# A planned GNN kernel: the planner's delay behind the GpSimd norm offsets, one planned cost, and the list of random moves are changed

## The chip, the cores and the metric

The kernel runs on one core of one Trainium2 chip. The metric is the device time of the whole program in microseconds. Three runs of the kernel before the change took 1513.4, 1514.27 and 1516.3 us; their median is 1514.27 us. A separate execution was recorded by the hardware profiler.

## What is computed

The input is 32 samples of 512 nodes with 128 features, and one adjacency matrix of 512 by 512 that all samples share. Four layers follow one another, each of them `x = x + layer(relu(layernorm(x)))`:

```python
    # layer 0: graph convolution
    A_hat = adj + eye; d = sum(A_hat, -1) ** -0.5
    out = einsum('nm,bmc->bnc', d[:, None] * A_hat * d[None, :], h) @ W.T + b
    # layer 1: gated graph network, five steps, in_matrix = out_matrix = adj
    m = einsum('nm,bmd->bnd', adj, h); av = concatenate([m, m])
    z = sigmoid(av @ w3.T + b3 + h @ u3.T + c3); r = sigmoid(av @ w4.T + b4 + h @ u3.T + c3)
    hv = tanh(av @ w5.T + b5 + (r * h) @ u5.T + c5); h = (1 - z) * h + z * hv
    # layers 2 and 3: graph attention over the edges of adj; layer 2 ends in elu
    h = x @ W; e = leaky_relu((h @ a_src)[:, None] + (h @ a_dst)[None, :])
    out = softmax(where(edge, e, -inf)) @ h
```

The layernorm has no learned scale: it is `(x - mean) / sqrt(var + eps)` over the 128 features. It stands ahead of every layer, so that there are four of them for each sample.

## The kernel before, in words

**Tiles.** A sample is one tile of 128 partitions by 4 chunks by 128 features (512 numbers in a partition). A product with the adjacency matrix (`in_three`, L682) and with the gate weights (`by_m`, L798) is done in three one-pass matmuls over an upper part, a lower part and a cross term. Between the second and the third of them ScalarE multiplies the accumulated PSUM bank by a constant (`rescale`, L664): TensorE can't go on in that bank until this is done. `operands` (L655 on ScalarE, L656 and L658 on VectorE) splits a value into the three parts. `weigh` (L795) holds the full-precision gate products, `step` the five steps of layer 1 (L828, L835 and L839 are their tanh on ScalarE; L830, L841, L842 and L844 are the elementwise work on VectorE), and `shuttle` and `shuttle_first` (L632, L642) turn a tile by a VectorE transpose and a pass through DRAM. `gat` is an attention layer: scores (L927), head values (L931), the masked exponentials on VectorE (L954), the weighted sum on TensorE (L980), its reciprocal (L983) and the residual (L987 to L1013).

**The norm.** `norm_relu` serves almost all norms. VectorE takes statistics of the four chunks (`bn_stats`, L546) and combines them (`bn_aggr`, L550). GpSimd then runs four operations on tiles of 128 by 4: variance plus eps (L558), its power -0.5 (L559), the negated mean (L560), and the product of the two last, the offset (`off`, L563). ScalarE then does one activation for each chunk: `relu(rstd * x + off)` (L565). Its output `y` or `h` goes to `operands`, to a VectorE transpose, or to a product. The first sample has a norm of its own (`norm_first`), and so have the attention layers of the last four samples (`center_relu`, L601 to L612): there ScalarE subtracts the mean only (L609), `aggr` (L605, L606) is on VectorE, and GpSimd's power (L612) is used later, on the attention scores.

**What sets the order.** Nothing runs in the order in which the Python code states it. Every operation is registered with `op(engine, cost, due, emit, r, w, delay)`: an engine, a cost in microseconds, a due time, what it reads and writes, and the delay from its end to the moment at which an operation that depends on it may start. Where no delay is given, one for each engine is used: 0.1 us for GpSimd, 0.145 for VectorE, 0.15 for ScalarE. `Plan.run` simulates the engines with these numbers: at each moment an engine takes, of its operations that are ready, the one with the smallest `soon`. It repeats the simulation ten times from each of two starting points, with `soon` replaced by the latest time that a backward pass allows, and keeps the best. Then `nudge` shifts the `soon` of some operations by the list `NUDGES`, `attempt` simulates once more, and the instructions are emitted in the order that comes out. On the chip each engine runs its own instructions strictly as emitted and waits on semaphores; the planner's times are not used there. Buffers are given out by the same simulation, so another order gives other buffers too.

**The random moves.** Each number of `NUDGES` stands for one move. A hash of it gives a window of planned time (20 to 800 us wide), the share of operations in the window that are touched, and how far their `soon` may be shifted at random, up or down:

```python
            width = 20 * 40 ** a
            begin, share, far = b * (end + width) - width, 65536 * 0.01 ** c, 0.02 * 100 ** d
```

One unit of `soon` is a slot of 9.7 us of planned time. The hash uses the number of the operation in the order of registration. Moves touch nothing that was planned in the first 12 us.

Of the kernel before, what the change touches and what calls it, by code (L numbers as in the profile page):

```python
# [14 lines left out]
ALU = mybir.AluOpType  # L15
# [14 lines left out]
WHOLE_GATES = {(0, 0), (1, 0)}  # L30

NUDGES = (
    582105, 147139, 36044, 562756, 451743, 52419, 574539, 43563, 131, 944493, 237051, 489767, 324034, 993924,
    895393, 724877, 242989, 757855, 969479, 343813, 441295, 487621, 599115, 887003, 965300, 304846, 630193,
    477347, 598911, 606866, 611222, 822063, 367989, 367611, 600045, 340292, 705911, 227256, 683560, 256619,
    236075, 331440, 177108, 65046, 739182, 728740, 720890, 134124, 359225, 176816, 49127, 311405, 367939,
    434468, 67122, 748109, 340066, 705658, 439275, 222157, 242131, 988248, 71674, 381732, 216141, 968473, 71317,
    32857, 119823, 447754, 129853, 185381, 116398, 835989, 550221, 241039, 261563, 95546, 93460, 950398, 27867,
    697942, 355550, 295201, 292698, 219542, 683929, 109572, 242409, 593734, 360934, 635653, 959394, 718615,
    571381, 736407, 37849, 298732, 275792, 981235, 444799, 634242, 442703, 439138, 943350, 210407, 114489,  # L40
    768468, 744083, 634443, 397291, 8136, 704668, 301010, 180477, 60933, 775473, 129214, 351397, 904571, 88879,
    916910, 435502, 757825, 84502, 678117, 887492, 424299, 920868, 742722, 635518, 887601, 436851, 937755,
    981183, 211427, 823433, 130707, 279663, 792970, 259083, 204724, 504719, 754655, 308189, 858342, 979517,
    719747, 751352, 82391, 821335, 468677, 957002, 276599, 466154, 75528, 451824, 370167, 884142, 189521,
    257883, 334963, 165897, 278684, 456540, 104146, 215128, 931617, 11886, 964863, 855753, 469785, 705445,
    36320, 949458,
)


# [29 lines left out]
class Plan:  # L79
# [13 lines left out]
    def op(self, engine, cost, due, emit, r=(), w=(), delay=None):  # L93
        o = Op(engine, cost, due, emit, self.DELAY[engine] if delay is None else delay)
        o.id = len(self.ops)
        before = {}
        for items, writes in ((r, False), (w, True)):
            for item in items:
                v, parts = item if isinstance(item, tuple) else (item, None)
                parts = range(len(v.writers)) if parts is None else [parts]  # L100
                if v not in o.vals:
                    o.vals.append(v)
                    v.uses += 1
                for c in parts:
                    before.update((p.id, p) for p in v.writers[c])
                    if writes:
                        before.update((p.id, p) for p in v.readers[c])
        for items, writes in ((r, False), (w, True)):
            for item in items:
                v, parts = item if isinstance(item, tuple) else (item, None)  # L110
                for c in range(len(v.writers)) if parts is None else [parts]:
                    if writes:
                        v.writers[c], v.readers[c] = [o], []
                    else:
                        v.readers[c].append(o)
        before.pop(o.id, None)
        for p in before.values():
            p.then.append(o)
        o.waits = len(before)
        self.ops.append(o)  # L120
# [190 lines left out]
def gnn_stack(ctx: ExitStack, tc: tile.TileContext, a: dict, out: bass.AP):  # L311
    nc = tc.nc
# [49 lines left out]
    op = plan.op  # L362
# [45 lines left out]
    for c in range(C):  # L408
        e, q = (("ACT", nc.scalar), ("SP", nc.sync))[c % 2]
        op(e, 0.45, -1001, lambda c=c, q=q: q.dma_start(adj_sb.t[:, c, :], adj[c * P:(c + 1) * P, :]),  # L410
           w=[adj_sb[c]], delay=(3.2, 4.7, 4.4, 4.9)[c])
# [42 lines left out]
    for m in range(C):  # L454
        op("DVE", 0.26, -800 + 0.7 * m, lambda m=m: nc.vector.tensor_add(diag.t[:, m, :], block(adjT.t, m), ident.t),
           r=[adjT, ident], w=[diag[m]])
# [67 lines left out]
    for k, u, half in (("w4", "u3", True), ("w3", "u3", True), ("w5", "u5", False)):  # L524
        gate_b[k] = fixed([P, 1], "gate_b" + k)
        op("DVE", 0.1, -14, lambda k=k, u=u: nc.vector.tensor_add(gate_b[k].t, raw["b" + k].t, raw["b" + u].t),
           r=[raw["b" + k], raw["b" + u]], w=[gate_b[k]])
# [4 lines left out]
    for i, l in enumerate((2, 3)):  # L532
        p = Val("bank")
        op("PE", 0.3, 9, lambda i=i, l=l, p=p: nc.tensor.matmul(p.t[:, 0, :2], gats.t[:, i, :], a_pair[l].t, start=True, stop=True),
           r=[gats, a_pair[l]], w=[p])
# [7 lines left out]
    def norm_stats(b, due):  # L543
        xb, st, mv = xs[b], Val("st", C), Val("mv")
        for c in range(C):
            op("DVE", 0.196, due, lambda c=c: nc.vector.bn_stats(st.t[:, c, :], xb.t[:, c, :]), r=[xb[c]], w=[st[c]])  # L546

        def aggr():
            for c in range(C):
                nc.vector.bn_aggr(mv.t[:, c, :], st.t[:, c, :])  # L550
        op("DVE", 0.29, due, aggr, r=[st], w=[mv])
        return mv

    def norm_relu(b, y, due, times=None):

        xb, off, rstd = xs[b], Val("off"), Val("rstd")
        mv = norm_stats(b, due)
        op("POOL", 0.5, due, lambda: nc.gpsimd.tensor_tensor(rstd.t, mv.t[:, :, 1], eps.t, ALU.add), r=[mv, eps], w=[rstd])  # L558
        op("POOL", 1.15, due, lambda: nc.gpsimd.tensor_tensor(rstd.t, rstd.t, mhalf.t, ALU.pow), r=[mhalf], w=[rstd])  # L559
        op("POOL", 0.42, due, lambda: nc.gpsimd.tensor_tensor(off.t, mv.t[:, :, 0], minus1.t, ALU.mult), r=[mv, minus1], w=[off])  # L560
        if times:
            op("DVE", 0.1, due, lambda: nc.vector.tensor_mul(rstd.t, rstd.t, times.t), r=[times], w=[rstd])
        op("POOL", 0.42, due, lambda: nc.gpsimd.tensor_tensor(off.t, off.t, rstd.t, ALU.mult), r=[rstd], w=[off])  # L563
        for c in range(C):
            op("ACT", 0.385, due, lambda c=c: nc.scalar.activation(  # L565
                chunk(y, c), xb.t[:, c, :], AF.Relu, bias=off.t[:, c:c + 1], scale=rstd.t[:, c:c + 1]),
               r=[xb[c], off, rstd], w=[y[c * len(y.writers) // C]])
# [27 lines left out]
    def center_relu(b, y, due):  # L595

        xb, st, mv, off, ve, rstd = xs[b], Val("st", C), Val("mv", 2), Val("off", 2), Val("ve"), Val("rstd")
        for a in range(2):
            both = slice(2 * a, 2 * a + 2)
            for c in (2 * a, 2 * a + 1):  # L600
                op("DVE", 0.2, due, lambda c=c: nc.vector.bn_stats(st.t[:, c, :], xb.t[:, c, :]), r=[xb[c]], w=[st[c]])  # L601

            def aggr(a=a, both=both):
                for c in (2 * a, 2 * a + 1):
                    nc.vector.bn_aggr(mv.t[:, c, :], st.t[:, c, :])  # L605
                nc.vector.tensor_scalar_mul(off.t[:, both], mv.t[:, both, 0], -1.0)  # L606
            op("DVE", 0.22, due, aggr, r=[st[2 * a], st[2 * a + 1]], w=[mv[a], off[a]])
            for c in (2 * a, 2 * a + 1):
                op("ACT", 0.385, due, lambda c=c: nc.scalar.activation(  # L609
                    y.t[:, c, :], xb.t[:, c, :], AF.Relu, bias=off.t[:, c:c + 1]), r=[xb[c], off[a]], w=[y[c]])  # L610
        op("DVE", 0.1, due, lambda: nc.vector.tensor_scalar_add(ve.t, mv.t[:, :, 1], EPS), r=[mv], w=[ve])
        op("POOL", 1.1, due, lambda: nc.gpsimd.tensor_tensor(rstd.t, ve.t, mhalf.t, ALU.pow), r=[ve, mhalf], w=[rstd])  # L612
        return rstd

    def chunk(h, c):
        return h.t[:, c, :]
# [119 lines left out]
    def gcn(pair, due):  # L736
        first, ys = pair[0] < 4, []
        for i, b in enumerate(pair):
            y = Val("y", C)
            if b == 0:  # L740
                norm_first(b, y)
            else:
                norm_relu(b, y, -797 if b == 1 else due + i, dinv if first else None)
            op("DVE", V, due + i + 3.8, lambda b=b: nc.vector.tensor_add(
                xs[b].t, xs[b].t, b0.t[:, None, :].to_broadcast([P, C, D])), r=[b0], w=[xs[b]])
            ys.append(y)
# [24 lines left out]
    def ggnn(b, due):  # L771
        lane, h, hT = Val("lane"), Val("h", C), Val("hT", Q)
        op("SP", 0.0, due - 3, lambda: None, r=[xs[b]], w=[lane], delay=0)
        op("SP", 0.0, due - 3, lambda: None, r=[lane], w=[h], delay=0)
        norm_relu(b, h, due - 2)
        if FAR0 <= b < B - FAR1:
            shuttle_first(h, hT, due - 2.5, due - 3)
        else:
            p = to_features(h, due - 2, hT)
            op("ACT", COPY, due - 2, lambda hT=hT: nc.scalar.copy(flat(hT.t), flat(p.t)), r=[p], w=[hT])  # L780
        turned = False
        for s in range(STEPS):
            now = due + LANES * s
            split = (b, s) not in WHOLE_GATES
            m = product(h, now, False) if (b, s) in WHOLE else in_three(h, turned, factors["adj"], now, split)
            if b == 4 and s == 0:
                op("SP", 0.0, now, lambda: None, r=[m[0] if split else m], w=[third], delay=0)
            h, turned, hT = step(b, s, m, hT, now, lane)
# [286 lines left out]
```

## Time and profile before

| what | value |
|---|---|
| median of three runs | 1514.27 us (1513.4 to 1516.3) |
| the profiled execution's own time | 1510.13 us |
| its span, from the first to the last instruction | 1508.2 us |
| granted TensorE clock | 1.000 |
| TensorE matmuls busy | 1494.0 us, 99% |
| VectorE busy | 1446.5 us, 96% |
| ScalarE busy | 1258.1 us, 83% |
| GpSimd busy | 294.6 us, 20% |
| mean of one L558, L559, L560, L563 on GpSimd | 456, 1206, 363, 437 ns, 119 of each |

Busy time is the union of an engine's instructions, without those that only wait or issue a DMA. Matmuls are pipelined and their ends are modelled in the profile, so that a busy TensorE may still be held up for a moment. A line such as L563 is a line of the kernel before. Idle time is put down to the instruction whose semaphore came last.

### The profile page before, as it was taken

Reading aid. Unit: us, or ns where it says so; the run is one execution under the profiler, and the core shown is the slowest. Engines: PE = TensorE matmul, PEld = TensorE weight load, DVE = VectorE, ACT = ScalarE, POOL = GpSimd, SP = SyncE. Lnnn points to the kernel's source line nnn. Section 1 sums busy time; section 2 is a strip of 40 time slices with the busy share of each in tenths; the row PEclk is TensorE's granted clock in tenths of the full one; section 3 lists DMA queues with packets and bytes.
Section 4 is the critical chain, followed back from the end, with each engine's and each line's share of the span. In section 5 each row is a group of like instructions: output and inputs, shape, how many; then the busy total and the mean of one; then the engine's idle time right before and its main releaser. Section 6 shows DMA issues by size and latency. Waiting matters only on the chain. (4 is left out here: it accounts for less than half of the span.)

```text
span 1508.2 us, 25120 instructions
## 1 busy us (share of the span) xinstructions
PE 1494.0 (99%) x7416; PEld 1160.5 (77%) x7416; DVE 1446.5 (96%) x3465; ACT 1258.1 (83%) x2781; POOL 294.6 (20%) x496
## 2 busy tenths in 40 slices
PE   9999999999999999999999999999999999999998
PEld 7677777777777877777777777777777877777888
DVE  8999989999999999999999999999989999998999
ACT  6788888888988898878888888888878798978874
POOL 4512111110212011321122212212211101110111
PEclk9999999999999999999999999999999999999999
DMA  3134334445444454434444434544344443442201
GB/s 112 35 86 118 84 84 106 121 129 129 111 122 102 106 130 132 105 94 111 126 127 103 125 101 123 125 110 134 95 109 126 108 132 93 111 113 70 58 29 50
DMA packets 270153, 157.78 MB, mean 105 GB/s; under 512 B 81248, under 2 KB 236224, under 8 KB 270016
## 3 DMA queue, kind: packets, MB, share of 16 engines
q1 hardware_dynamic: 269728, 155.66, 40.0%
q8 instruction: 58, 0.95, 0.3%
q14 instruction: 79, 0.65, 0.1%
q10 hardware_dynamic: 288, 0.52, 0.1%
HBM read 86.25 MB, written 69.84 MB: 103 GB/s over the span
## 5 line engine op out<-in xcount | busy, mean ns | idle before, releaser
L664 ACT ACTIVATE bank<-bank 128x512 f32<-128x512 f32 x819 | 464.9, 595 | 85.2 <-PE bank L682 59.2
L798 PE MATMUL bank<-upper,gates 128*128 128x512 f32 x474 | 232.9, 491 | 0.4 <-ACT bank L664 0.2
L658 DVE SCALAR_TENSOR_TENSOR across<-lower,upper 128x512 fp32r<-128x512 f32 x345 | 230.6, 677 | 2.7 <-PE bank L798 0.9
L980 PEld LDWEIGHTS bank<-h_gat,e 128*128 128x128 f32 x1792 | 218.1, 191 | 16.1 <-issue 7.9
L558 POOL TENSOR_TENSOR rstd<-mv,eps 128x4 f32<-128x4 f32 x119 | 54.3, 456 | 894.9 <-DVE mv L550 842.7
L980 PE MATMUL bank<-h_gat,e 128*128 128x129 f32 x1792 | 220.7, 275 | 0.0
L798 PE MATMUL bank<-across,gates 128*128 128x512 f32 x474 | 217.7, 473 | 0.0
L682 PE MATMUL bank<-adj,across 128*128 128x512 f32 x636 | 188.8, 420 | 2.7 <-DVE across L658 1.4
L682 PE MATMUL bank<-adj,upper 128*128 128x512 f32 x636 | 189.0, 418 | 0.0
L798 PE MATMUL bank<-lower,gates 128*128 128x512 f32 x474 | 186.7, 394 | 0.0
L682 PE MATMUL bank<-adj,lower 128*128 128x512 f32 x636 | 174.1, 395 | 0.0
L795 PE MATMUL bank<-hT,wT 128*128 128x512 f32 x320 | 163.3, 591 | 0.0
L795 PE MATMUL bank<-rh,wT 128*128 128x512 f32 x320 | 163.3, 592 | 0.0
L954 DVE SCALAR_TENSOR_TENSOR e<-row,h_gat,maskT 128x512 f32<-128x512 f32 x224 | 157.5, 742 | 0.0
L682 PEld LDWEIGHTS bank<-adj,across 128*128 128x128 f32 x636 | 117.4, 188 | 47.5 <-issue 14.4
L682 PEld LDWEIGHTS bank<-adj,upper 128*128 128x128 f32 x636 | 116.7, 188 | 38.1 <-issue 13.9
L559 POOL TENSOR_TENSOR rstd<-rstd,mhalf 128x4 f32<-128x4 f32 x119 | 143.5, 1206 | 1.3
L682 PEld LDWEIGHTS bank<-adj,lower 128*128 128x128 f32 x636 | 119.8, 188 | 28.2
L828 ACT ACTIVATE r<-bank,gate_bw 128x512 f32<-128x512 f32 x160 | 110.9, 695 | 24.2 <-PE bank L795 23.3
L565 ACT ACTIVATE y<-x,off,rstd 128x128 f32<-128x128 f32 x252 | 113.0, 497 | 15.4 <-POOL off L563 15.1
L798 PEld LDWEIGHTS bank<-across,gates 128*128 128x128 f32 x474 | 88.8, 188 | 45.2 <-ACT bank L664 19.9
L841 DVE TENSOR_TENSOR hv<-hv,hT 128x512 f32<-128x512 f32 x160 | 108.7, 681 | 13.6 <-ACT hv L839 13.4
(161 smaller groups left out, 2834.6 us busy)
## 6 DMA issues: line engine op xcount, KB each, us to landing
far<-sq SPq DMA_DIRECT2D x928, 64.0 KB
h<-far SPq DMA_DIRECT2D x148, 256.0 KB
gT<-far SPq DMA_DIRECT2D x56, 256.0 KB
row<-line SPq DMA_DIRECT2D x56, 256.0 KB
hT<-far SPq DMA_DIRECT2D x112, 64.0 KB
x<-in_x_dram SPq DMA_DIRECT2D x24, 256.0 KB
out_dram<-x SPq DMA_DIRECT2D x20, 256.0 KB
adjT<-in_x_dram SPq DMA_DIRECT2D x8, 256.0 KB
```

The costliest lines, as they stand in the source:

```text
L558: op("POOL", 0.5, due, lambda: nc.gpsimd.tensor_tensor(rstd.t, mv.t[:, :, 1], eps.t, ALU.add), r=[mv, eps], w=[rstd])
L559: op("POOL", 1.15, due, lambda: nc.gpsimd.tensor_tensor(rstd.t, rstd.t, mhalf.t, ALU.pow), r=[mhalf], w=[rstd])
L565: op("ACT", 0.385, due, lambda c=c: nc.scalar.activation(chunk(y, c), xb.t[:, c, :], AF.Relu, bias=off.t[:, c:c + 1], scale=rstd.t[:, c:c ...
L658: op("DVE", V, due - 5, lambda: nc.vector.scalar_tensor_tensor(flat(across.t), flat(lower.t).bitcast(F32), -SPLIT, flat(upper.t).bitcast(F ...
L664: op("ACT", COPY, due, lambda: nc.scalar.mul(flat(p.t), flat(p.t), by), w=[p])
L682: nc.tensor.matmul(flat(p.t), left.t[:, c, :], right.t[:, c, :], start=first and c == 0, stop=c == C - 1, skip_group_check=True)
L795: nc.tensor.matmul(flat(p.t), (of or gates).t[:, i, :], flat(moving.t), start=start, stop=True, skip_group_check=True)
L798: nc.tensor.matmul(flat(p.t), of.t[:, i - 1, :], flat(moving.t), start=start, stop=True, skip_group_check=True)
L828: op("ACT", A, due - 5, lambda: nc.scalar.activation(flat(r.t), flat(gate.t), AF.Tanh, bias=gate_b["w4"].t, scale=0.5), r=[gate, gate_b["w ...
L841: op("DVE", V, due - 5, lambda: nc.vector.tensor_sub(flat(hv.t), flat(hv.t), flat(hT.t)), r=[hT], w=[hv])
L954: op("DVE", 0.661, due + 3, lambda j=j: nc.vector.scalar_tensor_tensor(e.t[:, j, :], matrix(row), h.t[:, j, D + 1:D + 2], mask.t[:, j, :], ...
L980: nc.tensor.matmul(pt()[:, c, :D + 1], e.t[:, j, i * P:(i + 1) * P], h.t[:, j, :D + 1], start=(j == 0), stop=(j == C - 1))
```

## The change

Three things are changed; every instruction stays as it is, and their number too.

1. The offset operation on GpSimd (L563) gets a planned delay of 2.6 us instead of the engine's 0.1 us. In the planner, ScalarE's four activations of a norm become ready 2.5 us later than before.
2. `aggr` in `center_relu` gets a planned cost of 0.35 us instead of 0.22 us. It is registered twice for each of the two attention layers of the last four samples, 16 times in all.
3. `NUDGES` is replaced: 175 numbers are taken out, and 126 others put in.

The order on every engine is planned anew from these. The list is four lines shorter, so that what was L565 is L561 afterwards, and so on.

```diff
 NUDGES = (
-    582105, 147139, 36044, 562756, 451743, 52419, 574539, 43563, 131, 944493, 237051, 489767, 324034, 993924,
...
-    36320, 949458,
+    804225, 571398, 410389, 732559, 770994, 594527, 265916, 811198, 408600, 401627, 377811, 370275, 79629,
...
+    981916, 445563, 873345, 810508, 243250, 865339,
 )
@@ norm_relu
-        op("POOL", 0.42, due, lambda: nc.gpsimd.tensor_tensor(off.t, off.t, rstd.t, ALU.mult), r=[rstd], w=[off])
+        op("POOL", 0.42, due, lambda: nc.gpsimd.tensor_tensor(off.t, off.t, rstd.t, ALU.mult), r=[rstd], w=[off], delay=2.6)
@@ center_relu
-            op("DVE", 0.22, due, aggr, r=[st[2 * a], st[2 * a + 1]], w=[mv[a], off[a]])
+            op("DVE", 0.35, due, aggr, r=[st[2 * a], st[2 * a + 1]], w=[mv[a], off[a]])
```

## The prediction

> **What bounds the kernel now.** I read the page first, its busy times and costliest groups, then the waits engine by engine, then the timeline around TensorE's longest stops, and last the busy time by stretches near the end.
>
> ```profile
> PE 1494.0 (99%) x7416; PEld 1160.5 (77%) x7416; DVE 1446.5 (96%) x3465; ACT 1258.1 (83%) x2781; POOL 294.6 (20%) x496
> L664 ACT ACTIVATE bank<-bank 128x512 f32<-128x512 f32 x819 | 464.9, 595 | 85.2 <-PE bank L682 59.2
> L565 ACT ACTIVATE y<-x,off,rstd 128x128 f32<-128x128 f32 x252 | 113.0, 497 | 15.4 <-POOL off L563 15.1
> ```
>
> TensorE is busy for 1494.0 of 1508.2 us, and the change removes none of its work. So a new order can win at most the 14.2 us in which it isn't busy, and part of these are fixed: it starts at 1.1 us, and 3.1 us (1505.1 to 1508.2) lie after its last matmul. ScalarE is busy for 83%; its waits matter only where TensorE then waits for ScalarE. The waits of TensorE (columns: total, times, longest):
>
> ```profile
> PE bank L757 <- ACT m L710: 3.2, 2, 2.7
> PE bank L682 <- ACT bank L664: 2.8, 3, 1.5
> PE bank L682 <- DVE across L658: 1.4, 1, 1.4
> PE bank L442 <- DMA e<-in_adj_dram: 1.2, 2, 0.9
> PE bank L398 <- DVE hv L391: 1.1, 1, 1.1
> ```
>
> The last two lie in the first 7 us. The first three are what counts, and the timeline shows what lies behind each. Around 608 us:
>
> ```profile
> 605.48 3.10 POOL L558 TENSOR_TENSOR rstd<-mv,eps 128x4 f32<-128x4 f32 x1
> ...
> 607.83 0.69 DVE L658 SCALAR_TENSOR_TENSOR across<-lower,upper 128x512 fp32r<-128x512 f32 x1
> 608.43 0.71 DVE L632 STREAM_TRANSPOSE sq<-hT 128x512 f32<-128x512 f32 x1
> ...
> 608.76 1.65 ACT L565 ACTIVATE y<-x,off,rstd 128x128 f32<-128x128 f32 x4 [3.80 <-POOL off L563]
> ...
> 610.32 0.57 ACT L664 ACTIVATE bank<-bank 128x512 f32<-128x512 f32 x1
> ...
> 610.94 1.20 PE L682 MATMUL bank<-adj,across 128*128 128x512 f32 x4 [1.01 <-ACT bank L664]
> ```
>
> A GpSimd operation whose mean is 456 ns took 3.10 us. The activation that needs its norm stood at the head of ScalarE's queue for 3.80 us; the rescale that TensorE needed stood behind it; TensorE stopped for 1.01 us. The same chain shows at 843.37 (L563 took 3.02 us, ScalarE waited 3.07, TensorE stopped 1.51 at 847.24), at 1109.76 (L559 2.12 us, ScalarE 2.31, TensorE 1.44 at 1114.47, by way of L655 and L658), at 1397.01 (ScalarE 1.62, TensorE 0.24) and at 41.13 (L559 5.11 us, ScalarE 3.38, TensorE 2.72 at 43.96 for L710). Sum: 1.01 + 1.51 + 1.44 + 0.24 = 4.2 us in the steady part and 2.7 us at the start, 6.9 us in all.
>
> **What the Trainium skill says.** "SBUF — State Buffer", section "Who interferes with whom": a VectorE instruction with two SBUF inputs contends with a GpSimd instruction that reads SBUF, over a port pair that is locked for a whole instruction, and the loser blocks fully. The trace agrees: the 3.10 us operation spans L658, L842, L656, L844 and L658, all with two SBUF inputs and back to back, and ends at 608.58, 0.15 us after the one-input transpose L632 starts. So the lateness follows from VectorE's order, and a plan that prices GpSimd at fixed costs can't see it. "TensorE: Matmul & The Clock Gate", section "Architectural detail: the array is 16× 32×32, not 1× 128×128": ScalarE and VectorE take their queues strictly in order. The trace agrees: the L664 at 610.32 ran only after the waiting L565 at 608.76. "Perfetto Trace Analysis", section "GPSIMD Engine Instruction", warns that a GpSimd span is unreliable and that starts should be used; I rest on the ScalarE starts, which show the same lateness.
>
> **The change part by part.** *The delay, 0.1 to 2.6.* It puts nothing on the chip; it makes the planner place a norm's activations 2.5 us later behind the offset. GpSimd's four operations have means of 456 + 1206 + 363 + 437 ns = 2.46 us against planned 0.5 + 1.15 + 0.42 + 0.42 = 2.49, so the mean is right and the slack is for the late ones. ScalarE waits for POOL off 18 times, 24.6 us in all (19.2 for y, 5.4 for h). Of these waits the longest is 3.80, and 2.5 us of other ScalarE work put in front would leave 1.3 of it. The 3.80 cost TensorE only 1.0, so some 2.8 us of lateness are absorbed already: a rest of 1.3 costs TensorE nothing. I count all 4.2 us of the steady part as gone. At the start 3.38 - 2.5 = 0.9 us of waiting remain, and L710 may still stand behind the h activations (1.65 us) and L655 (0.63); I count half, 1.3 of 2.7, with both ends 0 and 2.7 in the range. What is moved with it: y's consumers (L655, L632, L642) go up to 2.5 us later in the ScalarE and VectorE queues, and the far and h transfers on SP with them, but only for norms that the plan ran close: I matched each offset to the next group of activations, and only 17 of 119 groups begin within 2.5 us of theirs; the median lag is over 20 us. For the other norms the delay changes nothing by itself. Cover if it fails: VectorE waits only 6.4 us in all for y or h.
>
> *aggr, 0.22 to 0.35.* In the trace its two L605 and one L606 start at 1410.51 and the next VectorE instruction at 1410.87: 0.36 us. So the plan becomes true here; 16 x 0.13 = 2.1 us of planned VectorE time that was missing in the last 100 us. Direct cost: nothing, since no instruction changes. The order it improves is VectorE's at the end; I take 0, with ends of -1 and +1.
>
> *The list of moves.* This reshuffles every queue after 12 us and is the part that no row prices. Bounds: TensorE's waits after 45 us that don't come from GpSimd sum to 0.4 (45 to 1400) and 0.7 (after 1400), that is 1.1 us. A new order can at best save these, and at worst strike as many bad coincidences as the GpSimd ones were, 6.9 us or more. I charge one such sum again, 1.0 us.
>
> Sum: -4.2 - 1.3 + 0 + 1.0 = -4.5 us. Against the profiled execution: span 1508.2 to 1503.7, its own time 1510.13 to 1505.6. The runs shown have a median 4.14 us above the profiled execution; I carry this over unchanged: 1514.27 - 4.5 = 1509.8 us, 0.30% less.
>
> **The rivals.** *More is gained (1505.4).* The start's 2.7 goes fully (6.9), the new order costs nothing, and half of the 4.1 us by which the timed runs exceed the profiled one is the same kind of lateness: -8.9. For it: such lateness is a matter of VectorE coincidences. Against it: the runs differ little among themselves (1513.4 to 1516.3).
>
> *Nothing is seen (1514.3).* The 5.5 us are saved, but the new order makes new stops of about 5.5 us, of the same chain with another releaser: ScalarE also waits 26.1 us in 29 waits for L983 and 59.2 us for L682 and, unlike L563, these keep their planned delays. Against it: in this trace they cost TensorE almost nothing.
>
> *Slower (1518.8).* The end is VectorE's, not TensorE's:
>
> ```profile
> 1300.00:1350.00 50.00, 49.98 (x247) 38.28 (x246) 47.80 (x97) 43.19 (x93) 4.87 (x8) 1.00 0.40 104
> 1350.00:1400.00 50.00, 49.76 (x239) 38.01 (x238) 44.63 (x101) 41.49 (x90) 6.92 (x12) 1.00 0.30 86
> 1400.00:1450.00 50.00, 49.95 (x315) 42.02 (x314) 47.55 (x134) 40.89 (x105) 8.52 (x11) 1.00 0.17 44
> ```
>
> The third busy time is VectorE's. From 1300 to 1450 it idles 2.2 + 5.4 + 2.5 = 10.0 us, and from 1450 to 1500 only 0.4. What it doesn't do before 1450 is added to the end. Its longest wait there by sum is the transpose L632 for L565, 2.7 us in 3 waits, and these activations are what the change plans later. If the new order doubles that idle time, 10.0 - 5.5 = +4.5 us result. It decides from 5.5 us of further idle time on, over 15.5 us in this stretch. Against it: eight groups of L565 lie there, and only two waited for GpSimd (2.0 us).
>
> **How the numbers follow.** The forecast (1507 to 1511.2) has 0.36, more gained 0.14, nothing seen 0.25, slower 0.25. About 0.2%, or 3 us, is what a measurement of this kernel can tell from no change: faster means under 1511.2, slower over 1517.3. So faster 0.50, same 0.25, slower 0.25. Range: the low end is all 6.9 and all of the 4.1 us, 1514.27 - 11.0 = 1503.3. The high end is the slower case with its idle time up by some 12 us, 1520.5; a tenth is left out on either side. The forecast's own range is 1507 to 1511.2.
>
> **What would show it.** Lines are four lower afterwards. Right: waits of ScalarE's L561 for GpSimd's L559 fall from 24.6 us to under 6, none over 2 us; no TensorE stop over 1 us between 45 and 1400 us; TensorE's idle time falls from 14.2 to about 10 us. GpSimd operations of 2 to 5 us remain, but nobody queues behind them. The start is right if the stop of 2.7 us for L710 is halved or gone. Wrong: TensorE's waits for L660 stay near 2.8 us or grow with another releaser behind them (nothing seen), or VectorE idles over 15.5 us in the 150 us that end 58 us before the end (slower).

## The result, and the profile after

In the first comparison the changed kernel took 1503.41 us (1502.18 to 1504.4, 4 runs) against 1513.84 us before (1512.93 to 1516.3, 4 runs): ratio 0.9928, 95% interval 0.9911 to 0.9945, or 10.4 us less. Beside a larger number of runs of the kernel before, the changed kernel took 1502.09 us (5 runs) against 1510.19 us (20 runs): ratio 0.9944, interval 0.9931 to 0.9956, or 8.1 us less. 4.5 us less were forecast. The profiled execution took 1502.88 us, with a span of 1501.0 us against 1508.2.

The page of the kernel after (first its busy times, then two groups with busy time, mean of one, and the idle time before them):

```profile
PE 1494.3 (100%) x7430; PEld 1162.3 (77%) x7430; DVE 1447.3 (96%) x3465; ACT 1261.3 (84%) x2781; POOL 285.9 (19%) x496
L660 ACT ACTIVATE bank<-bank 128x512 f32<-128x512 f32 x819 | 461.1, 593 | 93.1 <-PE bank L678 63.2
...
L561 ACT ACTIVATE y<-x,off,rstd 128x128 f32<-128x128 f32 x252 | 112.4, 496 | 0.2 <-POOL off L559 0.2
```

TensorE's idle time fell from 14.2 to 6.7 us. L561 (L565 before) had 15.4 us of idle time ahead of it in this form and has 0.2. TensorE's 14 more matmul records are 14 additional transposes (L357), which the planner puts into gaps near the end (1481 to 1484 us here); so, other than the section on the change says, the number of instructions isn't quite the same. They come to 1.5 us at 0.11 us from start to start, and count as busy time where there would be idle time.

The waits of ScalarE for GpSimd's offset, and all waits of TensorE in the kernel after:

```profile
ACT y L561 <- POOL off L559: 3.9, 3, 2.0
```

```profile
PE bank L394 <- DVE hv L387: 1.1, 1, 1.1
PE bank L794 <- ACT bank L660: 0.7, 2, 0.5
PE bank L962 <- DVE e L950: 0.6, 2, 0.4
PE bank L530 <- ACT wT L494: 0.5, 1, 0.5
PE bank L753 <- ACT m L706: 0.5, 1, 0.5
PE bank L678 <- ACT bank L660: 0.3, 1, 0.3
```

18 waits with 24.6 us have become 3 with 3.9 us, and no stop behind an offset is longer than 0.5 us. GpSimd itself is hardly quicker (busy for 285.9 us against 294.6). This is the longest case in the timeline of the kernel after:

```profile
812.26 4.16 POOL L556 TENSOR_TENSOR off<-mv,minus 128x4 f32<-128x4 f32 x1 [15.20 <-DVE mv L546]
...
817.73 0.61 POOL L559 TENSOR_TENSOR off<-off,rstd 128x4 f32<-128x4 f32 x1
...
818.37 0.88 ACT L561 ACTIVATE y<-adjT,off,rstd 128x128 f32<-128x128 f32 x2 [1.99 <-POOL off L559]
```

The four operations took 6.1 us in place of some 2.5, and ScalarE waited 1.99 of them. Six GpSimd operations of a norm last over 2 us in this trace, as many as before; ScalarE stands close behind two of them, this one and one at 699.08 us (4.17 us long, a wait of 1.8 us). Of the 119 groups of activations 8 begin within 2.5 us of their offset, 17 before.

**Lag.** The idle column shows only part of what TensorE loses, since the ends of matmuls are modelled. So I laid the starts of all matmuls against a sum of undisturbed intervals from start to start, taken from the traces themselves: 0.2325 us for a one-pass matmul of 512 columns, 0.429 us for each half of a full-precision one, 0.11 us for 128 columns. The time by which a start is later than this sum is called the lag here. It only grows, and its growth in a stretch is what TensorE lost there, visible as idle or not. How much it grows in one kernel depends a little on the intervals taken (by about 1 us over the run); differences between kernels don't:

| lag in us at | 45 | 350 | 700 | 1050 | 1400 | last matmul |
|---|---|---|---|---|---|---|
| before | 6.9 | 7.6 | 9.9 | 12.3 | 15.5 | 19.2 |
| after | 4.3 | 4.4 | 4.9 | 7.2 | 7.6 | 10.5 |
| before, early offsets (early_before) | 5.1 | 5.1 | 5.1 | 5.6 | 6.0 | 9.6 |
| after, early offsets (early_after) | 4.3 | 4.4 | 5.0 | 5.2 | 5.3 | 8.2 |

From before to after: 2.6 us less at the start, 8.6 - 3.3 = 5.3 us less from 45 to 1400, 3.7 - 2.9 = 0.8 us less at the end, from which the 1.5 us of the additional transposes have to be taken off, since they are part of the sum and not of the lag. That is 7.2 us, the difference of the spans.

### The profile page after: what moved, and what is told of

Its sections match the earlier page's. It is cut to its first block, busy times and chain, and to the rows that moved or that the text cites. A ratio compares the mean times of both kernels' runs of the same rounds, so it can differ in the third digit from the quotient of the medians.

```text
span 1501.0 us, 25160 instructions
## 1 busy us (share of the span) xinstructions
PE 1494.3 (100%) x7430; PEld 1162.3 (77%) x7430; DVE 1447.3 (96%) x3465; ACT 1261.3 (84%) x2781; POOL 285.9 (19%) x496
## 4 chain that ended last, share of the span: by engine, by line
PE 93%; DVE 4%; ACT 1%; POOL 1%; issue 1%; DMA 0%; SPq 0%; DVEq 0%; POOLq 0%
PE bank L678 33%; PE bank L794 21%; PE bank L791 18%; PE bank L976 12%; PE bank L907 3%; PE bank L753 2%; PE bank L962 1%; PE bank L703 1%; DVE e L950 1%; PE bank L620 1%; DVE across L654 0%; DVE lower L652 0%; POOL rstd L554 0%; POOL off L556 0%; PE bank L394 0%
## 5 line engine op out<-in xcount | busy, mean ns | idle before, releaser
L976 PEld LDWEIGHTS bank<-h_gat,e 128*128 128x128 f32 x1792 | 220.2, 191 | 23.6 <-issue 15.4
L794 PE MATMUL bank<-upper,gates 128*128 128x512 f32 x474 | 229.2, 484 | 0.0
L678 PEld LDWEIGHTS bank<-adj,upper 128*128 128x128 f32 x636 | 117.1, 188 | 37.1 <-issue 12.2
L555 POOL TENSOR_TENSOR rstd<-rstd,mhalf 128x4 f32<-128x4 f32 x119 | 133.6, 1123 | 1.1
L831 ACT ACTIVATE z<-bank,gate_bw 128x512 f32<-128x512 f32 x160 | 110.7, 692 | 19.2 <-PE bank L794 18.8
L651 ACT ACTIVATE upper<-bank 128x512 fp32r<-128x512 f32 x158 | 95.3, 603 | 33.0 <-PE bank L678 23.9
```

Source lines behind the costliest of these rows:

```text
L651: op("ACT", COPY, due - 5, lambda: nc.scalar.mul(made(upper.t), given(src.t), BELOW), r=[src], w=[upper])
L678: nc.tensor.matmul(flat(p.t), left.t[:, c, :], right.t[:, c, :], start=first and c == 0, stop=c == C - 1, skip_group_check=True)
L794: nc.tensor.matmul(flat(p.t), of.t[:, i - 1, :], flat(moving.t), start=start, stop=True, skip_group_check=True)
L831: op("ACT", A, due - 5, lambda: nc.scalar.activation(flat(z.t), flat(gate.t), AF.Tanh, bias=gate_b["w3"].t, scale=0.5), r=[gate, gate_b["w ...
L976: nc.tensor.matmul(pt()[:, c, :D + 1], e.t[:, j, i * P:(i + 1) * P], h.t[:, j, :D + 1], start=(j == 0), stop=(j == C - 1))
```

## The experiments

Two theories stood at the beginning. *Lateness*: norms that the plan ran close are late on the chip, and all that queues behind them on ScalarE is late; the longer delay removes this. *Draw*: the new list drew an order that happens to stall less, and the delay is worth little. The runs were made in four sets, each on one chip beside the kernel before, and a ratio is to the kernel before of the same set. The medians of the kernel before were 1509.7 to 1511.3 us in these sets, so that a difference between medians of two sets is uncertain by 1 to 2 us; where it matters, the ratios are compared as well.

### Empty lists

```diff
-NUDGES = (
...
-)
+NUDGES = ()
```

The rest of either kernel stays. no_list_prompt has the old delay and cost:

> The kernel before with an empty list of moves: delay 0.1 us behind the offset, aggr 0.22 us. Theory 1 (lateness: norms that the plan ran close are late on the chip, and all that queues behind their activations on ScalarE is late with them) expects the same lateness as in the kernel before, plus what the list had won: 1516 to 1524 us. Theory 2 (draw: the new list drew an order that happens to stall less, and the delay is worth 4.5 us at most) expects about the same, 1514 to 1524 us; the two are told apart by the next run.

Measured: 1505.77 us, ratio 0.9963 (0.9950 to 0.9975). Neither theory has this: without the list the kernel before is 5.5 us faster. no_list_late has the new delay and cost:

> The kernel after with an empty list of moves: delay 2.6 us, aggr 0.35 us. Theory 1 expects it faster than the one with an empty list and the short delay by 6 us or more, and to have no TensorE stop over 1 us that comes from a GpSimd offset. Theory 2 expects the two within 4 us of each other.

Measured: 1505.36 us, ratio 0.9960 (0.9947 to 0.9972): the same. Its waits of ScalarE for offsets are 2.0 us against 15.2, as lateness has it, but the time isn't less. The first theory in its plain form falls.

### The same orders with early offsets

Left out of each norm on GpSimd: the power and the negation.

```diff
-        op("POOL", 1.15, due, lambda: nc.gpsimd.tensor_tensor(rstd.t, rstd.t, mhalf.t, ALU.pow), r=[mhalf], w=[rstd])
-        op("POOL", 0.42, due, lambda: nc.gpsimd.tensor_tensor(off.t, mv.t[:, :, 0], minus1.t, ALU.mult), r=[mv, minus1], w=[off])
+        op("POOL", 1.15, due, lambda: None, r=[mhalf], w=[rstd])
+        op("POOL", 0.42, due, lambda: None, r=[mv, minus1], w=[off])
...
-        op("POOL", 0.42, due, lambda: nc.gpsimd.tensor_tensor(off.t, off.t, rstd.t, ALU.mult), r=[rstd], w=[off])
+        op("POOL", 0.42, due, lambda: nc.gpsimd.tensor_tensor(off.t, mv.t[:, :, 0], rstd.t, ALU.mult), r=[rstd], w=[off])
```

The planner sees the same costs, so every engine keeps its order; the traces show the same sequence on TensorE, VectorE and ScalarE, instruction by instruction. The offset now comes some 1.6 us ahead of its planned time, not just on time.

> The order of the kernel before, instruction by instruction, but GpSimd leaves out the power -0.5 and the negation in the norms: it does two of its four operations, and the offset is ready some 1.6 us earlier by the means, and by up to 5 us where the power was held up. Theory 1: with the offsets early the old order is good, 1503 to 1507 us. Theory 2: the order is what is worse, 1510 us or more.

Measured: 1501.60 us, ratio 0.9936 (0.9922 to 0.9949), 9.7 us less. So the old order, untouched, is good when offsets are early: in it, lateness costs up to 10 us. GpSimd is busy for 182 us less as well, which might relieve VectorE, but VectorE's busy time fell by 1.0 us only (1446.5 to 1445.5). The page says where the gain shows and where it doesn't:

```profile
PE 1491.2 (100%) x7416; PEld 1160.9 (77%) x7416; DVE 1445.5 (96%) x3465; ACT 1259.4 (84%) x2781; POOL 112.5 (8%) x258
```

The span fell by 9.6 us (1508.2 to 1498.6), TensorE's idle time by 6.8 only (14.2 to 7.4): the other 2.8 us were part of its busy time before.

> The order of the kernel after with the same two GpSimd operations left out of each norm. Both theories: within 1.5 us of the kernel after (1503.4), since its order leaves room for late offsets. A gain over 2 us would mean that late offsets still cost something after the change.

Measured: 1500.63 us, ratio 0.9929 (0.9916 to 0.9941). Against 1502.09 us for the kernel after, in the next set:

> The kernel after once more, beside the runs below, since the kernel before ran 2.5 us faster in the last set than in the first comparison (1511.3 against 1513.8 us). Both theories: 1501 to 1504 us.

Measured: 1502.09 us. Late offsets still cost the new order something: 1.5 us by these medians of two sets, 2.3 us by the ratios (0.9944 and 0.9929) and by the spans (1501.0 and 1498.7 us).

> The order of the kernel before with an empty list of moves, and the GpSimd power and negation left out of the norms as before. The empty list alone made the kernel before 5.5 us faster (1505.8 against 1511.3). Theory 1: the old list is a gain in an order whose offsets are on time and was lost to late ones, so this run is at least 2 us slower than the old list with early offsets (1501.6): 1503.5 to 1505.5. Rival: the old list is a loss in itself, and this run is at 1501.6 or under.

Measured: 1501.83 us, ratio 0.9943 (0.9930 to 0.9955). This falls between the two expectations and refutes the first: with early offsets, the old list is worth 0.2 us by the medians and 1.1 by the ratios, whose intervals overlap, not 2. What the list did on the chip was mainly to make late offsets dearer: 9.7 us with it, 1505.77 - 1501.83 = 3.9 without (3.0 by the ratios).

> Delay 2.6 us, aggr 0.35 us, empty list, and the GpSimd power and negation left out of each norm. With the full norms this order took 1505.4 us. If the longer delay takes nearly all of the lateness away (theory 1), early offsets gain under 1.5 us here: 1504 to 1505.4, and this order is itself some 2 to 3 us worse than the others with offsets on time (1500.6 to 1501.8). If lateness costs here what it costs with the short delay (4.0 us), it is 1501.5.

Measured: 1504.21 us, ratio 0.9968 (0.9957 to 0.9979). Against 1501.83 us with the short delay, this order is some 2.4 us worse in itself; the intervals of the two ratios don't overlap. What late offsets cost in it isn't settled: 1.2 us by the medians (1505.36 and 1504.21), 2.0 by the spans (1503.9 and 1501.9), nothing by the ratios (0.9960 and 0.9968). By the medians, the delay and the planned cost together took away 2.7 us of lateness and, without their list, gave 2.4 us back as a worse order.

### Later offsets

One more power ahead of each offset, into a tile that nobody reads; again the planner doesn't know, and the sequence on the other engines is the same. The new kernel keeps its `delay=2.6`. Lines are one higher than without the power.

```diff
+    again = fixed(SMALL, "again")
...
-        op("POOL", 0.42, due, lambda: nc.gpsimd.tensor_tensor(off.t, off.t, rstd.t, ALU.mult), r=[rstd], w=[off])
+        op("POOL", 0.42, due, lambda: (nc.gpsimd.tensor_tensor(again.t, rstd.t, mhalf.t, ALU.pow), nc.gpsimd.tensor_tensor(off.t, off.t, rstd.t, ALU.mult)), r=[rstd], w=[off])
```

> The kernel before in its own order, with one more GpSimd power (about 1.2 us, into a tile that nobody reads) ahead of each offset: every offset is some 1.2 us later, and the planner doesn't know. Theory 1, as it stands now (the old order pays for late offsets, with or without the list; the new order has room for them): 5 us or more slower than the kernel before. Theory 2 (late offsets matter little, the order itself differs): under 2 us slower.

Measured: 1547.24 us, ratio 1.0238 (1.0220 to 1.0255): 37.1 us slower.

> The kernel after in its own order with the same additional GpSimd power. Theory 1: under 2 us slower than the kernel after, since 2.5 us of room take 1.2 us of lateness. Theory 2: as much slower as the kernel before with it.

Measured: 1507.32 us, ratio 0.9979 (0.9971 to 0.9986): 5.2 us slower than the kernel after. More than expected, and a seventh of the loss of the old order. The waits of ScalarE for offsets, first in the old order, then in the new one, each with the power added:

```profile
ACT y L566 <- POOL off L564: 58.3, 46, 4.8
ACT h L566 <- POOL off L564: 10.5, 4, 4.4
```

```profile
ACT y L562 <- POOL off L560: 6.5, 6, 3.4
ACT h L562 <- POOL off L560: 0.6, 1, 0.6
```

The waits grew from 24.6 us to 58.3 + 10.5 = 68.8 us in the old order, and from 3.9 to 7.1 us in the new one. The added power took 1.2 us in the mean in both traces (1223 and 1242 ns).

Not all of the 37 us is waiting. After four of the long stops in extra_before, TensorE was granted half its clock for 3.4 us. The first of them, with the time before and during it (the number after the five busy times is the granted clock):

```profile
41.90:45.30 3.40, 0.00 (x0) 0.00 (x0) 0.41 (x1) 2.71 (x7) 0.62 (x2) 1.00 0.00 0
45.30:48.70 3.40, 3.31 (x12) 3.02 (x13) 3.40 (x13) 1.62 (x4) 2.67 (x4) 0.50 0.02 5
```

Within these four stretches the lag grew by 1.0 to 1.3 us each, 4.6 us together; extra_after has one such stretch with 1.2 us, and extra_no_list, below, one with 1.1. The kernels before and after have none ahead of their last matmul in the profiled executions. Is the difference between 37 and 5 us due to the delay or to the list?

> Short delay, empty list, one more GpSimd power (some 1.2 us) ahead of each offset, which the planner doesn't know. The kernel before lost 37 us by it, the kernel after 5 us. Theory 1 (the delay decides, not the list): a loss of 15 us or more against 1505.8, so over 1520. Rival (the old list is what makes the order frail): a loss of under 8 us, as for the kernel after.

Measured: 1537.81 us, ratio 1.0198 (1.0179 to 1.0216): 32.0 us over the same order without the power.

> The same with delay 2.6 us and aggr 0.35 us, empty list. Theory 1: at most 6 us over 1505.4. Rival (the new list is what makes the kernel after robust): as much as with the short delay.

Measured: 1511.49 us, ratio 1.0015 (1.0009 to 1.0022): 6.1 us over. So the room comes from the delay: 32 and 37 us without it, 6 and 5 us with it, whatever the list. By the ratios the two empty lists lost 35 and 8 us, which says the same. The planned cost of `aggr` was changed with the delay in these pairs; no run with the added power takes the two apart.

### The parts of the change alone

Three runs with an empty list change only the planned cost; 0.22, 0.35 and 0.48 us stand in their names:

```diff
-            op("DVE", 0.35, due, aggr, r=[st[2 * a], st[2 * a + 1]], w=[mv[a], off[a]])
+            op("DVE", 0.22, due, aggr, r=[st[2 * a], st[2 * a + 1]], w=[mv[a], off[a]])
```

> Delay 2.6 us, empty list, aggr back at 0.22 us: the changed cost alone, against 1505.4 us with 0.35. It touches 16 operations in the last 100 us; both theories: within 2 us of 1505.4, either way.

Measured: 1509.23 us, ratio 0.9995 (0.9987 to 1.0003), 3.9 us over the value 0.35. Neither theory had this.

> Empty list, short delay, aggr 0.35 us: the cost alone against 1505.8 us with 0.22. If the truer cost orders the end better, 1501 to 1504 us, gained after 1400 us. If the 3.9 us with the long delay were a draw of the order, anything from 1502 to 1510, with the difference spread over the run.

Measured: 1515.10 us, ratio 1.0031 (1.0022 to 1.0040): with the short delay the same cost makes it 9.3 us slower.

> Empty list, long delay, aggr 0.48 us, which is as much over the measured 0.36 us as 0.22 is under it. If a true cost matters, 1506 to 1509 us, with the loss after 1400 us. If each value is a draw, no relation to the distance from 0.36.

Measured: 1504.41 us, ratio 0.9963 (0.9951 to 0.9975). So the value's distance from the measured 0.36 us doesn't decide. A planned cost of the last 100 us changes the order of the whole run, because the planner's backward pass starts at the end: between 45 and 1400 us the lag grows by 4.3 us in no_list_prompt and by 11.2 us in no_list_prompt_035. Each value acts like another draw, and the five empty lists lie between 1504.4 and 1515.1 us.

Two more exchange the lists: the first is the kernel before with the new delay, shown here, the second the kernel after with the old one, the same edit backwards (its planned cost stays 0.35 us).

```diff
-        op("POOL", 0.42, due, lambda: nc.gpsimd.tensor_tensor(off.t, off.t, rstd.t, ALU.mult), r=[rstd], w=[off])
+        op("POOL", 0.42, due, lambda: nc.gpsimd.tensor_tensor(off.t, off.t, rstd.t, ALU.mult), r=[rstd], w=[off], delay=2.6)
```

> The kernel before with the delay of 2.6 us alone: old list, aggr 0.22 us. Theory 1 (the delay removes lateness, whatever the list): TensorE stops behind late offsets go, and the time is at or under the empty list with delay 2.6 us and aggr 0.22 us (1509.2): 1504 to 1509. Rival (a list fits only the plan that it was chosen for; in another plan it is noise): slower than the kernel before, 1512 to 1530 us, without waits for offsets.

Measured: 1520.17 us, ratio 1.0073 (1.0058 to 1.0087): slower than before, though ScalarE waits for offsets only twice (6.8 us). The lag at the last matmul is 26.8 us, spread over the run.

> The kernel after with the delay taken back to 0.1 us: new list, aggr 0.35 us. Theory 1 alone: 1505 to 1511, some 3 to 9 us of lateness over the kernel after. Rival (the list is noise in another plan): 1515 to 1535 us.

Measured: 1531.84 us, ratio 1.0142 (1.0129 to 1.0155). In both the rival in the expectations holds: a list fits the plan that it was chosen for. The moves are tied to the numbers of operations and to the planned times of one plan; in another plan they shift operations that were well placed. Against an empty list with the same delay and cost, the old list costs 10.9 us under the new delay, and the new list 16.7 us under the old one. Only in its own plan does the new list gain: 1505.36 to 1502.09 us, by the ratios (0.9960 to 0.9944) 2.4 us.

## Why the prediction was wrong

**What held.** The mechanism and its place: GpSimd's operations held up behind back-to-back two-input work of VectorE, ScalarE's strict order, TensorE at the end of the chain. The waits for offsets fell under 6 us (3.9), none over 2 us, no stop over 1 us remained between 45 and 1400 us, and the idle time fell below the 10 us named. The old order with early offsets, and both orders with later ones, show the cause on the chip. "Slower" is refuted: VectorE idles 50 - 48.04 + 50 - 46.12 + 50 - 48.12 = 7.7 us from 1300 to 1450, not over 15.5:

```profile
1300.00:1350.00 50.00, 50.00 (x226) 37.21 (x226) 48.04 (x93) 44.30 (x94) 4.04 (x8) 1.00 0.43 111
1350.00:1400.00 50.00, 50.00 (x279) 40.33 (x278) 46.12 (x109) 41.65 (x97) 5.94 (x9) 1.00 0.30 84
1400.00:1450.00 50.00, 50.00 (x306) 41.39 (x305) 48.12 (x124) 41.77 (x104) 6.87 (x10) 1.00 0.20 50
```

**The step that failed: "Sum: 1.01 + 1.51 + 1.44 + 0.24 = 4.2 us in the steady part".** This is what lateness costs in the idle column, and I took it for all of the cost. The bound in front of it, "at most the 14.2 us in which it isn't busy", has the same fault: with early offsets the same 7416 matmuls are busy for 1491.2 us, not 1494.0. With early offsets the lag of the old order between 45 and 1400 us grows by 0.9 us in place of 8.6: lateness cost 7.7 us there. The four stops come to 3.9 us of lag; 15 further stops of 0.1 to 0.4 us each come to 3.5 us, the rest are still shorter. Most of these lie under the modelled ends of matmuls. The stretches of the kernel before show it (the first number behind the length is TensorE's busy time):

```profile
350.00:700.00 350.00, 348.55 (x1724) 271.95 (x1723) 340.83 (x801) 296.81 (x654) 70.37 (x122) 1.00 0.45 115
700.00:1050.00 350.00, 348.49 (x1701) 269.39 (x1700) 340.81 (x799) 298.37 (x663) 73.07 (x123) 1.00 0.46 118
1050.00:1400.00 350.00, 348.31 (x1699) 268.53 (x1698) 332.45 (x735) 294.44 (x646) 53.20 (x92) 1.00 0.41 106
```

They show 4.7 us idle in the three together, while the lag grew by 7.9. Nor did all of the lateness go, as "I count all 4.2 us of the steady part as gone" has it: late offsets still cost the new order some 2.3 us there, where its lag grows by 3.3 us, and by 1.0 with early offsets.

**The start.** "I count half, 1.3 of 2.7": the lag at 45 us fell by 2.6 us, practically all. The half was a choice between 0 and 2.7 that the profile didn't settle.

**The list, +1.0.** It is worth -2.4 us in its own plan. But as a step by itself it has no price: the parts don't add. The delay with the old list is 10.2 us slower than before, the new list and cost with the old delay 21.9 us slower, all three together 8.1 us faster.

**aggr, "0, with ends of -1 and +1".** Wrong in its bounds: with an empty list, 3.9 us faster with one delay and 9.3 us slower with the other. I priced the instructions near the changed cost; the cost moves all of them.

**Sum by stretches.** Forecast: start -1.3, middle -4.2 + 1.0 = -3.2, end 0. Measured: -2.6, -5.3 and +0.7, that is -7.2 in the spans. That is 2.7 us more than forecast. The other 3.2 us that the forecast lacks against the first 10.4 come from a second step: "I carry this over unchanged", of the 4.14 us between the median and the profiled execution. The changed kernel's profiled execution lies only 0.5 us under its median, and in the later sets the kernel before had medians of 1509.7 to 1511.3 us, about its profiled 1510.13. So some 2 us of the first 10.4 us are of that set of runs alone; 8.1 us is the better figure. Both measured times lie outside the forecast's own range (1507 to 1511.2), the first just inside the wide one (from 1503.3), the second below it. "More is gained" (1505.4) came nearest, in part for its reasons: the start's stop did go fully, and the new order cost little. But it added half of those 4.1 us, where the steady part's short stops were missing; that the sum came near is in part luck.

**Open.** Why the orders differ with early offsets (1500.6, 1501.6, 1501.8 and 1504.2 us) was not settled. That the port pair is what holds GpSimd up was read from the timeline and from what the Trainium skill states ("SBUF — State Buffer", section "Who interferes with whom"); no run took the two-input work of VectorE away. The traces before and after speak for it: beside the norms' GpSimd operations that took over 0.6 us more than the shortest of their kind, 73 and 76% of VectorE's instructions have two SBUF inputs, and beside those that took under 0.1 us more, 27 and 26%.

## What to carry to other kernels

Where a static order meets an operation with a variable time, it is safer to plan it at its late end than at its mean: here 1.2 us more that the plan didn't foresee cost 32 to 37 us where the consumer was planned right behind, and 5 to 6 us where 2.5 us were left. This is room, and not yet a gain: with an empty list and the lateness as it was, the longer delay left the time where it was (1505.8 and 1505.4 us). The price of such waits is read from the starts of the bounding engine against its undisturbed intervals, because short stops hide in busy times. A list of moves, or any other tuning of one plan, has to be judged only together with the costs that it was made for.

## What had not been expected of the hardware

GpSimd's power of a 128 by 4 tile took between 1.00 and 5.11 us in one execution of the kernel before; beside the longest, VectorE ran seven instructions with two SBUF inputs in a row. After stops of TensorE of 2.0 to 3.8 us the granted clock was 0.5 for 3.4 us four times in extra_before, but not after the stop of 2.7 us in the profiled kernel before, nor after one of 3.2 us in new_list_prompt; what decides wasn't tested. In the four sets, 12 of the 81 executions of the kernel before show a mean granted clock of 0.998 or less and took 1511.7 us in the mean, the others 1509.8; so the clock explains part of the spread, and not the 8 us between the kernels.

The kernel before spread from 1506.2 to 1516.3 us over its runs, the kernel after from 1501.0 to 1504.4 us, and the early-offset order of the kernel after only from 1500.2 to 1501.0 us.
